# A residual's copy in quarters, and a transfer model in a kernel's own order account

## The chip, the cores and the metric

The kernel runs on one core of a Trainium2 chip. Its time is the device time of one execution in microseconds (us); what counts is the median of several runs. A core has TensorE (PE, matrix products; its weight loads are shown as PEld), VectorE (DVE), ScalarE (ACT), GpSimd (POOL) and SyncE (SP). Each works through its own instructions in order and waits on semaphores. Transfers (DMAs) are issued here by SP, POOL and at the start ACT, and all run on the same 16 DMA engines.

## The reference

Two layers over `x` of 8 images x 256 channels x 32 x 32, in float32. Layer 0 is a convolution and attention hybrid, layer 1 is full attention over the 1024 positions followed by eight experts. Cut to what matters:

```python
# layer 0; the residual is the x on the left
x = x + L0(_gn(x), ...)      # 1x1 products, pooled keys and values (1426 tokens), depthwise 3x3,
                             # layernorm, attention of 8 heads, global-token mix, projection
# layer 1
t = _to_tokens(x)
t = t + L1_attn(_ln_t(t), Wq, bq, Wk, bk, Wv, bv)
t = t + L1_ffn(_ln_t(t), ...)   # 8 experts, three products each, weighted by a softmax gate
x = _from_tokens(t, x)
```

So `t1 = x + L0(...)` is formed for each image, and layer 1 reads it.

## The kernel before

**Stages.** The first stage (to about 1945 us) runs the layer-0 attention of the eight images one after another. Each image `b` has four units, `(c, half)`: four heads `c`, 512 queries `half`. A unit has `NKC` = 12 steps over the keys. In a step PE makes the scores `sc` (four heads, one PSUM tile of four banks), ACT takes the exponential into a tile `pt` (128 x 2048, six buffers), and PE multiplies by the values into `pv`. For each pair of steps `add` (line 1501) has POOL issue a transfer that adds one `pt` to the other in SBUF (`accum_op`); `sums` (line 1508) has DVE add the pairs up, and `normalise` divides. After an image's fourth unit `project` (line 1535) makes the output product and has POOL add it with accumulating stores of 256 KB (`t<-xr`) into `t1[b]` in DRAM.

Everything else of that stage is put between the steps as filler: `prepare(b)` (line 1351) loads the image (`xi`, two halves of 512 KB), normalises, pools and projects it for the next image; `queries` stores `hn<-pool`; `layer1` (line 1599) loads `t1[b]` of a finished image into `t` (1 MB) and makes the second attention's scores and values; `outputs` loads `res`, stores `t2` and `hn`. From about 1970 us the experts run, first with the rest of layer 1 between them, then alone.

**The residual.** `t1[b]` must hold `x[b]` before `project` accumulates into it. For images 0 to 6 `prepare(b)` has SP issue one copy from DRAM to DRAM, 1 MB, right behind the loads of `xi` (lines 1356 and 1357). For the last image `project` loads `x` into SBUF and stores the sum.

**The order account.** The order of each engine's instructions is not written by hand. While the program is built, class `Flow` keeps an account of time: `now` is the time to which each engine is booked, `ready` when each tile is written, `read` when its readers are done. `note` (line 761) books every instruction with a cost from `cost` (line 721; a transfer's issue is 1.0 us on POOL, 0.4 us on SP). Generators (`prepare`, `layer1`, `sums` and so on) say before each piece which engine and tiles they need, and `runnable` (line 837) lets a piece in when the account says that its tiles are there in time: for PE by `at + MARGIN <= until` with `MARGIN` = 1.5, where `until` is about when the PSUM tile of the scores is free. `tile` picks the buffer that is free first. So a booked duration decides where instructions stand in each engine's fixed order; on the chip the engines follow that order and wait on the real semaphores.

For a transfer `note` adds a lag from the end of its issue to its landing, line 799: 2.0 + 0.0045 us for each KB (of 1000 bytes) on SP, 1.5 + 0.0078 on POOL. A transfer's lag doesn't depend on others that are under way.

**The main loop** stands at the end of `attention`: it goes over `steps` (line 1829), calls `scores`, lets filler in with `f.step`, calls `values` for the step before, and `add` after each odd step.

Of the kernel before, what the change touches and what calls it, by code (L numbers as in the profile page):

```python
# [14 lines left out]
DRAM = bass.MemoryType.DRAM  # L15

P = 128
# [7 lines left out]
NKC = 12  # L25
# [26 lines left out]
class Kit:  # L52


    def __init__(self, nc):
        self.nc = nc
        self.n = 0
# [598 lines left out]
class Flow:  # L656
# [27 lines left out]
    def __init__(self, tc, kit):  # L684
        nc = tc.nc
        self.tc, self.kit = tc, kit
        self.now = dict.fromkeys(("PE", "DVE", "ACT", "POOL", "SP"), 0.0)
        self.last = {}
        self.ready, self.read, self.writer, self.reader, self.slots, self.open = {}, {}, {}, {}, {}, set()
        self.pe = self.Engine(self, "PE", nc.tensor)  # L690
        self.ve = self.Engine(self, "DVE", nc.vector)
        self.act = self.Engine(self, "ACT", nc.scalar)
        self.pool = self.Engine(self, "POOL", nc.gpsimd)
        self.sp = self.Engine(self, "SP", nc.sync)
        self.threads = []
        self.cut = {}
        self.also = {}
        self.tiled = None
        self.columns = False
        self.credit, self.port = [0.0, 0.0], 0.0  # L700

    def tile(self, pool, shape, tag, bufs=1):
# [58 lines left out]
    def note(self, engine, op, ins, args, kwargs):  # L761
        aps = [a for a in (*args, *kwargs.values()) if hasattr(a, "tensor") or hasattr(a, "space")]
        out = kwargs.get("out", args[0] if args else aps[0])
        srcs = [a for a in aps if a is not out]
        prev = self.last.get(engine)
        if prev is not None:
            self.tc.add_manual_dep(
                ins.ins,
                prev,
                mybir.DependencyInfo(mybir.DependencyClass.NoSync, mybir.DependencyReason.DATA),  # L770
                reason="program order",
            )
        self.last[engine] = ins.ins.name
        start = self.now[engine]
        names = [n for a in srcs for n in self.keys(a)]
        outs = self.keys(out)
        for n in (*names, *outs):
            if self.writer.get(n) != engine:
                start = max(start, self.ready.get(n, 0.0))
        for o in outs:  # L780
            if self.reader.get(o, engine) != engine:
                start = max(start, self.read.get(o, 0.0))
        cost = self.cost(engine, op, out, srcs)
        if engine == "PE":

            tiling = None if op == "transpose" else self.tiling(srcs)
            if tiling != self.tiled:
                cost += {None: 0.2, "rows": 0.2, "columns": 0.13}[tiling]
                self.tiled = tiling

        wide = [a for a in srcs if a.space != PSUM and a.free_size() > 4]
        if "dma" not in op and engine == "POOL" or engine == "DVE" and wide and (len(wide) > 1 or op in ("tensor_scalar", "tensor_copy")):
            start = max(start, self.port)
            self.port = start + cost
        self.now[engine] = end = start + cost
        lag = 0.15
        if "dma" in op:
            size = 4e-3 * out.shape[0] * out.free_size() if out.space != DRAM else 4e-3 * srcs[0].shape[0] * srcs[0].free_size()
            lag = 2.0 + 0.0045 * size if engine == "SP" else 1.5 + 0.0078 * size
        for n in {*outs, self.key(out)}:  # L800
            self.ready[n] = max(self.ready.get(n, 0.0), end + lag)
            self.writer[n] = "DMA" if "dma" in op else engine
        self.open.difference_update(names)
        for n in {*names, *map(self.key, srcs)}:
            self.read[n] = max(self.read.get(n, 0.0), end + lag)
            self.reader[n] = engine

    @staticmethod
    def key(a):
# [85 lines left out]
def attention(tc, kit, f, outer, ended, nb, consts, x, t1, t2, hn, bounds, vecs, q_t, kv_t, proj_t, gqk_t, wqk, wqkv, vecs1, w1_d, w1c, gate_d, wrc, vecs2, bnvec):  # L895
# [6 lines left out]
    with ExitStack() as ctx:  # L902
        l1, shared = outer
        wp = ctx.enter_context(tc.tile_pool(name="w0", bufs=1))
        work = ctx.enter_context(tc.tile_pool(name="work0", bufs=1))
        psum = ctx.enter_context(tc.tile_pool(name="psum0", bufs=1, space=PSUM))

        def T(pool, shape, tag, bufs=1):
            return f.tile(pool, shape, tag, bufs=bufs)
# [157 lines left out]
        todo, done, read, freed, key_parts, normalised = [], [], [2], [0], [0], [0]  # L1067
# [283 lines left out]
        def prepare(b):  # L1351

            if b:
                yield until(lambda: len(asked) == 4)
            xi = xs.pop(b) if b in xs else load_x(b)
            if b < nb - 1:
                f.sp.dma_start(t1[b], x[b].rearrange("(k p) n -> p k n", p=P))
            st = T(work, [P, 2, 2, 6], "st")
            mv = T(work, [P, 2, 2], "mv")
            for k in range(2):  # L1360
                yield ve(xi[:, k, :])
                for h in range(2):
                    f.ve.bn_stats(st[:, k, h, :], xi[:, k, h * 512 : (h + 1) * 512])
                f.ve.bn_aggr(mv[:, k, :], st[:, k, :, :].rearrange("p h s -> p (h s)"))
            mean, var = mv[:, :, 0], mv[:, :, 1]
            yield pe(mv, tag="sm")
            gm = small()
            f.pe.matmul(gm[:, 0:2], lhsT=grp, rhs=mean, start=True, stop=True)
            yield ve(gm)
            mu = T(work, [P, 2], "mu")  # L1370
            f.ve.tensor_copy(mu, gm[:, 0:2])
            dev = T(work, [P, 2], "dev")
            f.ve.tensor_tensor(dev, mean, mu, ALU.subtract)
            f.ve.tensor_tensor(dev, dev, dev, ALU.mult)
            f.ve.tensor_tensor(dev, dev, var, ALU.add)
            yield pe(dev, tag="sm")
            gv = small()
            f.pe.matmul(gv[:, 0:2], lhsT=grp, rhs=dev, start=True, stop=True)
            yield ve(gv)
            gr = T(work, [P, 2], "gr")  # L1380
            rstd(gr, gv[:, 0:2], 1e-5)
            for k in range(2):
                yield ve(gr)
                f.ve.tensor_scalar(
                    xi[:, k, :], xi[:, k, :], mu[:, k : k + 1], gr[:, k : k + 1], ALU.subtract, ALU.mult
                )
            xl = T(work, [P, 2, NK - HW], "xl")
            if b == 0:
                f.spawn(pool_levels(xi, xl), 2)
            else:  # L1390
                yield from pool_levels(xi, xl)
            xp = xi, xl
            if b == 0:
                todo.extend([None] * 4)
                f.spawn(queries(b, xi), 3)
                yield from first_maps(xp)
            else:
                yield from maps(xp)
            if b:
                yield from queries(b, xi)  # L1400
            made[0] += 1
# [430 lines left out]
        for i in range(len(steps) + 1):  # L1832
            if i < len(steps):
                b, c, half, kc = steps[i]
                sl = slice(half * 512, half * 512 + 512)
                if kc % 4 == 0:
                    f.finish(lambda: key_parts[0] > 3 * b + kc // 4)
                if (half, kc) == (0, 0):
                    f.finish(lambda: (b, c) in qs and (b or (c, 0) in asked))
                    turn[0] = 2 * b + c  # L1840
                    atts[b, c] = T(work, [P, HW], "att", bufs=2)
                if i == 4:
                    f.finish(lambda: {0, 1}.issubset(whole))
                if b == 0 and kc == 0:
                    f.finish(lambda: (c, half) in asked)
                pts[i] = scores(b, c, sl, kc)
                f.step()
            if i:
                b1, c1, half1, kc1 = steps[i - 1]
                if kc1 == 0:  # L1850
                    pv = T(psum, [P, 512], "pv")
                    pairs = []
                    sl1 = slice(half1 * 512, half1 * 512 + 512)
                    f.spawn(unit(b1, c1, sl1, i // NKC, pairs), 0)
                f.finish(lambda: kc1 // 4 in vts[b1])
                values(b1, c1, kc1, pts[i - 1], pv)
                if kc1 % 2:
                    add(kc1, pts.pop(i - 1), pts[i - 2])
                    pairs.append(pts.pop(i - 2))
                if kc1 == NKC - 1:  # L1860
                    f.finish(lambda: projected[0] >= b1)
                    f.act.activation(atts[b1, c1][:, sl1], pv, AF.Copy)
            if i < len(steps):
                f.step((PACE, PACE1))
# [687 lines left out]
```

## Time and profile before

| what | value |
|---|---|
| median of 5 runs | 3311.89 us (3306.25 to 3312.99) |
| the profiled execution | 3312.69 us |
| its span, first to last instruction | 3310.9 us |
| mean granted TensorE clock | 0.978 |
| PE busy | 3103.3 us (94%) |
| DVE busy | 2470.5 us (75%) |
| ACT busy | 1736.0 us (52%) |
| POOL busy | 1220.0 us (37%) |
| transfers issued by POOL, whole span | 179.85 MB, 28.3% of the 16 engines |
| transfers issued by SP, whole span | 181.32 MB, 15.7% of the 16 engines |

The page shows one profiled execution. Its span is the time from the first to the last instruction; the run's own time is 1.8 us longer. Busy slices cut the span in 40 equal parts of 82.8 us and give each engine's busy share in tenths. In views of groups and waits, a line names the engine, the tile it writes, and what ended the idle time before it: `PE sc L669 <- ACT pt L669` means that PE sat idle before writing `sc` until ACT had done with `pt`. L669 is the line of the account's wrapper through which nearly all instructions are issued, so lines say little and tiles say much. A DMA's landing time runs from the start of its issue.

The seven copies of the residual were issued at 1.7, 36.5, 232.6, 409.4, 599.5, 801.4 and 1019.8 us. The four units of image 4, for example, begin at 1052.4, 1127.0, 1177.1 and 1234.3 us.

### The profile page before, as it was taken

The numbers are of one execution on the slowest core, as the hardware profiler recorded it, in microseconds if no ns is written. First come the engines' busy times: TensorE is split into PE (matmuls) and PEld (weight loads), VectorE is DVE, ScalarE is ACT, GpSimd is POOL, SyncE is SP. The second block draws the span as 40 slices with busy tenths as digits, with TensorE's granted clock in tenths as the row PEclk, the third lists the DMA queues.
The fourth block names the chain that finished last, engine by engine and source line by source line (L and its number), as shares of the span: only waits on it lengthen the run. The fifth ranks groups of instructions, "written<-read, shape, count | busy, mean of one in ns | idle before, by whom it ended". The sixth has DMA issues, their size and how long they took to land. (4 is left out here: it accounts for less than half of the span.)

```text
span 3310.9 us, 56919 instructions
## 1 busy us (share of the span) xinstructions
PE 3103.3 (94%) x22906; PEld 1794.4 (54%) x22906; DVE 2470.5 (75%) x4067; ACT 1736.0 (52%) x2329; POOL 1220.0 (37%) x1309
## 2 busy tenths in 40 slices
PE   8788879989999989999989889999999999999998
PEld 4322224334333434334334247777888888888887
DVE  5798989899789869877545545346888887787776
ACT  4466757576766666667565543333333333444443
POOL 2213241420422222211121211006765667777776
PEclk9798989999999999999999999999999999999999
DMA  2265664665655656656666655124444430000000
GB/s 75 70 167 116 137 145 97 136 147 121 131 134 133 121 128 133 135 114 127 145 137 130 135 155 198 58 83 166 140 153 147 143 125 26 20 20 32 20 13 21
DMA packets 111906, 366.89 MB, mean 111 GB/s; under 512 B 13632, under 2 KB 38984, under 8 KB 88400
## 3 DMA queue, kind: packets, MB, share of 16 engines
q0 software_dynamic: 28608, 179.85, 28.3%
q1 hardware_dynamic: 79664, 181.32, 15.7%
q8 instruction: 183, 3.00, 0.4%
q10 hardware_dynamic: 3360, 1.97, 0.2%
q14 instruction: 91, 0.75, 0.1%
HBM read 114.55 MB, written 83.40 MB: 60 GB/s over the span
## 5 line engine op out<-in xcount | busy, mean ns | idle before, releaser
L669 ACT ACTIVATE pt<-sc 128x2048 f32<-128x2048 f32 (+1 forms) x384 | 720.2, 1876 | 302.4 <-PE sc L669 228.4
L669 DVE SCALAR_TENSOR_TENSOR acc<-p,vec,acc 128x961 f32<-128x961 f32 (+3 forms) x960 | 571.4, 604 | 29.5 <-ACT acc L669 3.9
L669 PE MATMUL sc<-q,kn 32*128 32x512 f32 (+1 forms) x3072 | 447.0, 652 | 109.1 <-ACT pt L669 107.8
L669 DVE TENSOR_TENSOR pt<-pt,pt 128x1024 f32<-128x1024 f32 x320 | 387.2, 1254 | 130.9 <-DMA pt<-pt 130.3
L669 POOL DMA_DIRECT2D pt<-pt x192 | 172.9, 900 | 748.9 <-ACT pt L669 633.5
L669 PE MATMUL pv<-pt,vt 128*32 128x512 f32 (+1 forms) x3072 | 420.8, 620 | 1.4 <-ACT att L669 1.4
L669 ACT ACTIVATE p1c<-bank 128x256 f32<-128x256 f32 x229 | 87.5, 382 | 561.0 <-PE bank L669 554.9
L669 ACT ACTIVATE h<-h,bnvec 128x512 f32<-128x512 f32 x458 | 346.5, 805 | 63.0 <-DVE h L669 54.1
L669 POOL TENSOR_TENSOR rstd<-rstd,mhalf 128x4 f32<-128x4 f32 (+2 forms) x88 | 109.6, 1246 | 669.0 <-DVE rstd L669 628.0
L669 DVE TENSOR_TENSOR h<-p1c,bank 128x512 f32<-128x512 f32 x229 | 156.0, 681 | 220.6 <-PE bank L669 209.9
L669 PEld LDWEIGHTS sc<-q,kn 32*128 32x128 f32 (+1 forms) x3072 | 116.2, 178 | 317.2 <-ACT pt L669 206.9
L669 POOL TENSOR_TENSOR tm<-h,tm 128x256 f32<-128x256 f32 x208 | 239.6, 1152 | 16.3
L669 DVE TENSOR_TENSOR h<-u,bank 128x256 f32<-128x256 f32 x458 | 233.2, 550 | 7.9
L669 PEld LDWEIGHTS pv<-pt,vt 128*32 128x32 f32 (+1 forms) x3072 | 60.7, 108 | 304.5 <-issue 287.9
L669 POOL TENSOR_TENSOR tm<-h 128x512 f32<-128x512 f32 x104 | 136.9, 1316 | 195.1 <-ACT h L669 195.1
L669 DVE TENSOR_TENSOR h<-h,gate 128x1024 f32<-128x1024 f32 x128 | 201.6, 1575 | 0.5 <-ACT h L669 0.5
L669 PE MATMUL bank<-h,w2e 128*128 128x256 f32 (+1 forms) x608 | 196.4, 452 | 2.1 <-DVE h L669 1.2
L669 PE MATMUL y<-t,s3e 128*128 128x256 f32 x768 | 187.0, 379 | 4.0 <-POOL t L669 2.1
L669 PE MATMUL bank<-t,s1e 128*128 128x256 f32 x750 | 182.5, 379 | 0.2 <-DVE h L669 0.2
L669 PE MATMUL sm<-y,t 128*32 128x256 f32 (+1 forms) x2144 | 178.7, 382 | 1.4 <-ACT p L669 1.4
L669 PE MATMUL sm<-p,v 128*32 128x256 f32 (+1 forms) x2088 | 177.6, 379 | 0.0
L669 POOL TENSOR_TENSOR t<-h,t 128x256 f32<-128x256 f32 x214 | 170.9, 799 | 16.8
(313 smaller groups left out, 5420.9 us busy)
## 6 DMA issues: line engine op xcount, KB each, us to landing
pt<-pt POOLq DMA_DIRECT2D x160, 1024.0 KB, 7.7
h<-h SPq DMA_DIRECT2D x126, 512.0 KB, 3.3
xi<-in_x_dram SPq DMA_DIRECT2D x16, 512.0 KB, 8.2
t<-t SPq DMA_DIRECT2D x8, 1024.0 KB, 9.3
res<-t SPq DMA_DIRECT2D x32, 256.0 KB, 4.7
t<-res SPq DMA_DIRECT2D x32, 256.0 KB, 4.1
hn<-res SPq DMA_DIRECT2D x32, 256.0 KB, 4.7
hn<-hn SPq DMA_DIRECT2D x16, 512.0 KB, 4.8
```

Of the source, the lines that this page charges most:

```text
L669: ins = fn(*args, **kwargs)
```

## The change

The copy goes out of `prepare`. In the main loop, at step 6 of each unit's 12, SP now issues a quarter: the 128 channels `c` and the 512 positions of that unit, 256 KB, DRAM to DRAM, for images 0 to 6. That makes 28 transfers instead of 7, each of the same image whose unit is running.

In the account the lag of a transfer is no longer fixed. `transfer` keeps two numbers, the work in us that is still left on SP's queue (with the few that ACT issues) and on POOL's. Work is 0.0048 us a KB for POOL's transfers and for those from DRAM to DRAM, 0.0026 for others. Since the last call, `served`, time has gone by: while both queues hold work each is served at half rate, then the one that is left at the full rate. The lag is 1.7, plus what is left on the own queue with the new transfer, plus as much of the other queue's as is served meanwhile; for a transfer that is booked earlier than `served`, the difference is added.

```diff
@@ Flow.__init__
         self.columns = False
+        self.left, self.served = [0.0, 0.0], 0.0
         self.credit, self.port = [0.0, 0.0], 0.0
@@ Flow.note
         lag = 0.15
         if "dma" in op:
+            both = out.space == DRAM and srcs[0].space == DRAM
             size = 4e-3 * out.shape[0] * out.free_size() if out.space != DRAM else 4e-3 * srcs[0].shape[0] * srcs[0].free_size()
-            lag = 2.0 + 0.0045 * size if engine == "SP" else 1.5 + 0.0078 * size
+            lag = self.transfer(engine, end, size * (0.0048 if engine == "POOL" or both else 0.0026))
@@ Flow
+    def transfer(self, queue, at, work):
+
+        span = max(0.0, at - self.served)
+        self.served = max(self.served, at)
+        mine, other = queue == "POOL", queue != "POOL"
+        left = self.left
+        both = 2 * min(left)
+        done = min(span, both) / 2
+        for i in range(2):
+            left[i] = max(0.0, left[i] - done - max(0.0, span - both))
+        left[mine] += work
+        return 1.7 + left[mine] + min(left[mine], left[other]) + self.served - at
@@ prepare(b)
             xi = xs.pop(b) if b in xs else load_x(b)
-            if b < nb - 1:
-                f.sp.dma_start(t1[b], x[b].rearrange("(k p) n -> p k n", p=P))
             st = T(work, [P, 2, 2, 6], "st")
@@ the main loop of attention
                     atts[b, c] = T(work, [P, HW], "att", bufs=2)
+                if kc == NKC // 2 and b < nb - 1:
+                    f.sp.dma_start(t1[b][:, c, sl], x[b, c * P : (c + 1) * P, sl])
                 if i == 4:
```

## The prediction

> **What bounds the kernel now.** I read the page's busy slices first, then the waits of each engine in the attention stage (75 to 1945 us), then stretches of some 30 us where the transfers are thick, then the transfers themselves.
>
> ```profile
> PE   8788879989999989999989889999999999999998
> PEclk9798989999999999999999999999999999999999
> DMA  2265664665655656656666655124444430000000
> ```
>
> PE sets the end: 3103.3 of 3310.9 us are busy, and behind slice 24 (about 2000 us) it hardly idles. The transfers, which are all that this change touches, are thick in slices 2 to 23 only, which is the attention stage. So what can be won or lost is PE's idle time before 2000 us, with the slow clock that follows on it. PE's waits from 75 to 1990 us say what ends that idle time, and the waits of ACT, DVE and POOL (75 to 1945 us) what stands behind:
>
> ```profile
> PE sc L669 <- ACT pt L669: 107.8, 91, 4.4
> ...
> PE sx L669 <- DVE st L669: 8.6, 1, 8.6
> ```
>
> ```profile
> ACT pt L669 <- DMA pt<-pt: 46.9, 15, 5.2
> ...
> DVE pt L669 <- DMA pt<-pt: 127.0, 42, 8.0
> ...
> DVE st L669 <- DMA xi<-in_x_dram: 12.2, 2, 8.1
> ...
> POOL rstd L669 <- DVE rstd L669: 420.2, 72, 15.3
> ```
>
> Columns: total us, times, longest. PE waits for an exponential (`pt`), and the exponential in 15 cases for a `pt` buffer that an accumulating transfer still holds. Where this bites is seen in six stretches (busy us of each engine, then granted clock, share of the DMA engines, GB/s):
>
> ```profile
> core 0: us, PE busy (x) PEld busy (x) DVE busy (x) ACT busy (x) POOL busy (x), PEclk, DMA share, GB/s
> ...
> 409.00:439.00 30.00, 18.48 (x120) 5.97 (x116) 17.48 (x30) 12.36 (x11) 2.59 (x3) 0.83 0.86 224
> 597.00:627.00 30.00, 28.35 (x268) 11.29 (x264) 25.32 (x55) 17.23 (x20) 8.16 (x10) 1.00 0.86 201
> ...
> 1186.00:1216.00 30.00, 22.29 (x158) 7.42 (x154) 17.59 (x42) 20.37 (x23) 8.91 (x11) 0.94 0.78 167
> ...
> 1872.00:1902.00 30.00, 21.05 (x176) 5.34 (x176) 13.37 (x12) 13.98 (x9) 8.29 (x9) 0.83 0.64 128
> ```
>
> 409 and 597 are places of the residual's copy: one loses 11.5 us of PE, the other 1.7 (at 799 and 1018 it is 0 and 0.4). The stretches at 1186 and 1872, and two like them at 1424 (24.46 busy) and 1662 (22.27), hold no copy; together they lose 7.7 + 5.5 + 7.7 + 9.0 = 29.9 us. The stretch from 445 to 480, behind the clash at 409, has PE busy 23.80 of 35: 11.2 lost. POOL shows how the late ones begin:
>
> ```profile
> 1196.79 0.71 POOL L669 TENSOR_TENSOR rstd<-rstd,mhalf 128x2 f32<-128x2 f32 x1 [9.65 <-DVE rstd L669]
> 1197.47 0.88 POOL L669 DMA_DIRECT2D pt<-pt  x1
> ...
> 1198.70 1.19 POOL L669 DMA_DIRECT2D pt<-pt  x1
> ```
>
> POOL stood 9.65 us for a late DVE; two accumulating transfers queued behind it went out 1.2 us apart, the second took 12.4 us, and the exponentials ran out of buffers (4.05 and 3.12 us). It is an error of the written order: the account had DVE earlier than it was.
>
> **The change part by part.** Sizes and landing times in the attention stage:
>
> ```profile
> pt<-pt POOLq DMA_DIRECT2D x160, 1024.0 KB, 7.7
> hn<-pool SPq DMA_DIRECT2D x28, 256.0 KB, 3.5
> ...
> t<-t SPq DMA_DIRECT2D x7, 1024.0 KB, 9.7
> ...
> xi<-in_x_dram SPq DMA_DIRECT2D x12, 512.0 KB, 8.3
> ...
> t<-in_x_dram SPq DMA_DIRECT2D x5, 1024.0 KB, 14.6
> ```
>
> *Issue.* Seven copies become 28 quarters. A copy took 977 ns to issue, a 256 KB store (`t<-res`) 526: 28 x 0.53 - 7 x 0.98 = +8 us on SP, which stood 581 us for `res` alone in this stage. Cost on the path 0; uncovered, 0.5 us of delay for one load a unit. Nothing new waits: the accumulating stores of `project` (first at 362.8 us) need the quarters of their image, the last of which goes out in the middle of its fourth unit (about 313 us for image 0). If that cover went, POOL would stand at line 1557 and the `pt` transfers behind it.
>
> *Copy gone from the head of `prepare`.* At 409 the load of 1 MB `t` (405.0), `hn`, two `xi` and the copy meet three `pt` transfers; the second half of `xi` came 20 us after its issue and DVE, then PE, stood 8.6 us. The copy is queued behind `xi`, so its removal alone need not bring `xi` forward (at 597, with a copy behind, `xi` took 7.5). But the account changes too: it had given each `xi` 2.0 + 0.0045 x 524 = 4.4 us. Now it has 1.7, plus what SP still holds (by then about 4.5: the rest of `t` and `hn`, and 1.36 for each `xi`), plus as much again while POOL holds some (3): some 9 us. PE's matmul then comes 4.6 us later in the order, with other work ahead. Bounds 0 and -11.5; I take -5, nearest to those 4.6. At the start (copies at 1.7 and 36.5 us) PE's first matmul at 8.87 waits for `mv`; I take 0.
>
> *Shorter accumulations in the account.* Before: 1.0 issue + 1.5 + 0.0078 x 1049 = 10.7 us. Now 1.0 + 1.7 + 0.0048 x 1049 = 7.7, more when SP holds work; measured 7.7. The additions in `sums` come some 3 us earlier in DVE's order, and buffers count as free sooner. No row prices an order not yet written; the bounds are the idle time of the stretches that began so, -41.1 (29.9 + 11.2), and the loss in the rival below. The 445 to 480 stretch follows from the clash at 409, so I give back most of it, -8, and of the four others a fifth, -6, since their cause (a late `rstd`) is only indirectly touched.
>
> *Quarters in the middle of units.* Beside a 1 MB copy two `pt` transfers took 9.4 to 12.5 us instead of 7.7, so a copy costs 3.4 to 9.6 us of their lateness, a quarter 0.9 to 2.4. Mostly there is slack; but the stretches at 1186, 1424 and 1662 lie at steps 2 to 10 of a unit, and there the quarter lands: 3 x 0.9 to 2.4 = +2.7 to +7.2. I take +4.
>
> *Loads that now look quicker.* `t` of 1 MB: 7.1 us in the account before, now 0.4 + 1.7 + 2.73 = 4.8, or 7.5 while POOL transfers; measured 9.7, and PE's margin is 1.5. Extra lateness 0 to 2.3 us for 7 loads; with half the time covered by POOL and filler work at hand I take +3 (0 to +16). The weights at 1971 (PE idle 10.1 us there for `w2e`) get 2.8 instead of 3.6: 0, between -3 and +3.
>
> Sum: -5 - 8 - 6 + 4 + 3 = -12. The profiled run has a span of 3310.9 and took 3312.69, 0.8 above the median 3311.89; so 3298.9 us of span, and a median of 3300.
>
> A page against the change: the Trainium skill, "DMA: Bandwidth & Descriptors", section "Bandwidth", says to "Batch DMAs to ≥1 MiB for ≥75% of peak"; its fixed 2.0 us for each DMA ("Anatomy of one DMA") would make four quarters some 6 us dearer than one copy, an estimate, 42 us over the run, all in SP's queue; by it the sum would stay unless those us reach the three tight units. The same fit gives an accumulation 2.0 + 2.4 = 4.4 us, where the row says 7.7; by the page even the new account would be 3 us too slow and the rival below would fall, but the row decides.
>
> **Rivals.** *Slower: the cushion is gone.* The account was 3 us too long for the accumulations, and still DVE waited for them 42 times. At 7.7, the median, half of them come later than written; DVE, in order, stands, the statistics behind it are late, POOL stands at `rstd`, and the next transfers go out in pairs as at 1197. For it: the 420.2 us of `rstd` waits. Against: the account now lengthens an accumulation when SP is busy, which the long ones are. Such a stretch costs 29.9 / 4 = 7.5 us of PE. The other terms being -5 - 8 + 4 + 3 = -6, two more stretches decide (+9). With one more in each of three images that have none: -6 + 22.5 = +16, so 3328.
>
> *No change: transfers were hidden anyway.* Only 46.9 us of ACT's waits are on transfers; filler not done beside them is done after 2000 us at the same price. The clash at 409 is relieved (-5), the quarters cost their lower end (+2.7), the loads nothing: -2.3, so 3310.
>
> *It doesn't do what it says.* SP is in order and stood up to 115.9 us for one store (`hn<-pool`); a quarter behind such a wait is issued with the next burst, as the copy was. Then the quarters cost their upper end, +7.2, beside the -5 of the account: +2, so 3314.
>
> **How the numbers follow.** Forecast (3286 to 3305) 0.47, cushion gone 0.33, hidden 0.14, bunched 0.06. Only about 0.2% (6.6 us) can be told from no change here. Faster 0.48 takes in a little of the hidden case; same 0.19; slower 0.33. The range 3283 to 3332 leaves out the far ends of the first two, about 2 in 10.
>
> **What would show it.** The wait of PE for DVE `st` (8.6) gone and PE busy over 24 in the stretch after the fourth image's `xi` load; the 445 to 480 stretch above 30 of 35. ACT's waits on `pt` transfers under 46.9 if the account helps, over it if the cushion mattered; POOL's pairs of transfers 1.2 us apart fewer or more than the four. DVE's wait on transfers above 200 us would speak for the rival. No SP issue of `t<-in_x_dram` beside `xi`, but 28 spread over the units. I am wrong if PE's idle time before 2000 us grows.

## The result, and the profile after

The changed kernel takes 3316.72 us (median of 30 runs, 3307.32 to 3324.98); beside it the kernel before took 3309.41 us (51 runs). The ratio is 1.0021, with a 95% interval of 1.0015 to 1.0026: 7 us slower, where 12 us faster was forecast. The profiled execution has a span of 3318.7 us, 7.8 above that of before.

The page after, busy slices of PE, the granted clock and the DMA engines:

```profile
PE   8787889999989999989989989999999999999998
...
PEclk9799899999999999999999999999999999999999
DMA  1365655645665565566766746224444440000000
```

PE is as full as before. Its busy time grew by 10.4 us (3103.3 to 3113.7), and its idle time, the sum of the gaps between matmuls, fell from 199.1 to 195.6. What grew can be split at the events that both traces show. The first exponential starts at 83.5 us instead of 81.6 and the last ends at 1954.9 instead of 1943.7: the attention stage is 9.2 us longer. The first expert product comes at 1989.5 instead of 1976.9, and the store of the gate (`gtd`) at 2250.9 instead of 2238.3, both 12.6 late. Of these 12.6 some 5 come back behind the gate, because more expert work was done by then: PE is busy for 1044.9 us from that store to the end, instead of 1049.6.

In the attention stage PE's idle time fell too, 158.2 to 155.0 us, and its busy time grew by 12.5. Part of this is the clock: matmuls that began while half of it was granted take 108.5 us of the stage instead of 89.0 (a `sc` matmul has 0.24 us then, instead of 0.13). At the full clock these 19.5 us more would have taken about half as long, so in this pair of executions some 10 us, an estimate, go with the clock. That the loss as such is the clock isn't shown. Over all executions on record the granted clock has a mean of 0.9783 for the changed kernel (32) and of 0.9789 for the one before (113, beside the experiments), which is some 2 us of a span. In two more draws of the changed kernel (e9 and e10 below) it was 0.0016 and 0.0015 lower than beside them, but with the copy whole (e1 below), which is as slow as the change, 0.0009 higher.

Waits in the attention stage after (75 to 1955 us; total, times, longest):

```profile
PE sc L669 <- ACT pt L669: 118.9, 112, 3.9
```

```profile
ACT pt L669 <- DMA pt<-pt: 35.2, 11, 5.4
```

```profile
DVE pt L669 <- DMA pt<-pt: 177.3, 82, 8.0
```

```profile
POOL rstd L669 <- DVE rstd L669: 442.8, 70, 19.2
```

ACT waits less for a `pt` buffer (46.9 before), DVE much more for an accumulated pair (127.0, 42 times before): the additions stand earlier in DVE's order than their transfers land. The stretches, first after and then before (columns as in the prediction: PE, PEld, DVE, ACT and POOL busy, then granted clock, share of the DMA engines, GB/s):

```profile
405.00:440.00 35.00, 28.24 (x210) 7.97 (x210) 32.03 (x56) 20.32 (x21) 8.63 (x8) 0.95 0.88 209
445.00:480.00 35.00, 33.99 (x322) 12.65 (x318) 28.63 (x33) 19.91 (x20) 22.65 (x26) 0.93 0.50 110
...
930.00:960.00 30.00, 22.96 (x176) 7.49 (x172) 29.23 (x54) 18.60 (x14) 10.54 (x11) 0.97 0.86 185
...
1440.00:1470.00 30.00, 21.92 (x142) 6.49 (x146) 24.49 (x61) 19.19 (x22) 9.65 (x10) 0.89 0.75 158
```

```profile
405.00:440.00 35.00, 21.82 (x148) 7.01 (x148) 22.06 (x45) 15.71 (x12) 2.99 (x4) 0.85 0.86 215
445.00:480.00 35.00, 23.80 (x156) 5.31 (x160) 34.36 (x39) 17.47 (x14) 24.41 (x27) 0.80 0.68 143
```

```profile
930.00:960.00 30.00, 28.34 (x295) 12.37 (x288) 24.19 (x36) 20.17 (x27) 6.33 (x8) 1.00 0.55 138
1440.00:1470.00 30.00, 25.33 (x166) 7.91 (x162) 15.75 (x24) 21.17 (x28) 8.70 (x7) 0.94 0.60 120
```

The clash at the fourth image's load is gone: PE was busy 21.82 of the 35 us from 405 before, now 28.24, and 23.80 of those from 445, now 33.99. New thin stretches came in other places, with a lower clock (930: 5.4 us less PE, 0.97 instead of 1.00). The transfers (KB each, median us to landing):

```profile
pt<-pt POOLq DMA_DIRECT2D x160, 1024.0 KB, 7.7
t<-in_x_dram SPq DMA_DIRECT2D x28, 256.0 KB, 6.5
...
t<-t SPq DMA_DIRECT2D x7, 1024.0 KB, 7.2
...
xi<-in_x_dram SPq DMA_DIRECT2D x12, 512.0 KB, 5.5
```

Loads of `xi` and `t` land sooner (8.3 and 9.7 before), the accumulations as before. SP's queue around the fourth image's load, after and then that load before:

```profile
424.16 0.84 SPq L669 DMA_DIRECT2D xi<-in_x_dram  x2
425.04 0.50 SPq L669 DMA_DIRECT2D t<-in_x_dram  x1
442.90 0.34 SPq L669 DMA_DIRECT2D q<-hn  x1
443.30 1.17 SPq L669 DMA_DIRECT2D t<-in_x_dram  x1
444.52 1.00 SPq L669 DMA_DIRECT2D res<-t  x1
```

```profile
406.78 2.60 SPq L669 DMA_DIRECT2D xi<-in_x_dram  x2
```

Most quarters don't go out in the middle of the units. All 28 follow the SP transfer ahead of them by 0.04 to 0.06 us: a quarter waits for nothing, so SP issues it as soon as the wait ahead of it is over. Beside the exponential of step 6 that is up to 65 us early (243.9 instead of 309.0), and in one case 0.5 late; 11 of the 28 are within 5 us of it.

### The profile page after: what moved, and what is told of

It reads as the page before. It is cut to its first block, busy times and chain, and to the rows that moved or that the text cites. A ratio compares the mean times of both kernels' runs of the same rounds, so it can differ in the third digit from the quotient of the medians.

```text
span 3318.7 us, 56921 instructions
## 1 busy us (share of the span) xinstructions
PE 3113.7 (94%) x22888; PEld 1795.0 (54%) x22888; DVE 2463.4 (74%) x4066; ACT 1735.1 (52%) x2328; POOL 1205.8 (36%) x1303
## 3 DMA queue, kind: packets, MB, share of 16 engines
q1 hardware_dynamic: 82368, 183.42, 16.2%
## 5 line engine op out<-in xcount | busy, mean ns | idle before, releaser
L669 PE MATMUL sm<-p,v 128*32 128x256 f32 (+1 forms) x3048 | 223.0, 381 | 0.2 <-DVE gr L669 0.2
L669 PEld LDWEIGHTS sm<-p,v 128*32 128x32 f32 (+1 forms) x3048 | 141.3, 118 | 92.1 <-issue 32.7
L669 POOL TENSOR_TENSOR t<-h 128x512 f32<-128x512 f32 x106 | 137.0, 1293 | 106.7 <-DVE h L669 83.9
```

The costliest lines, as they stand in the source:

```text
L669: ins = fn(*args, **kwargs)
```

## The experiments

Ratios are to the kernel before, run on the same chip beside them, with 95% intervals. "Booked" is the account's time from the issue of a 1 MB accumulation to its landing: 1.0 for the issue and the lag.

**The two parts alone.** e1 takes `after` and puts the whole copy back behind the `xi` load; e2 takes `before`, with the quarters in the loop:

```diff
 e1: new account, copy whole
+            if b < nb - 1:
+                f.sp.dma_start(t1[b], x[b].rearrange("(k p) n -> p k n", p=P))
-                if kc == NKC // 2 and b < nb - 1:
-                    f.sp.dma_start(t1[b][:, c, sl], x[b, c * P : (c + 1) * P, sl])
 e2: old lags, copy in quarters
-            if b < nb - 1:
-                f.sp.dma_start(t1[b], x[b].rearrange("(k p) n -> p k n", p=P))
+                if kc == NKC // 2 and b < nb - 1:
+                    f.sp.dma_start(t1[b][:, c, sl], x[b, c * P : (c + 1) * P, sl])
```

> The new account with the copy whole, at the head of prepare. Theory A (the account loses: accumulations booked at 7.7 us put DVE's additions too early): about +7 us against the kernel before, ratio 1.002, DVE's wait on pt transfers near 177 us as in the changed kernel. Theory B (the quarters lose, by meeting the accumulating transfers in the middle of units): ratio 1.000 or below, since the xi load is booked better. Theory C (any new order draws anew, whatever the transfers do): anywhere within 0.997 to 1.004, and not the sum of parts.

> The old lags with the copy in quarters at the middle of units. Theory A: ratio 1.000 or below, the clash at the fourth image's load relieved, DVE's wait on pt transfers near 127 us. Theory B: about 1.002, and longer waits of exponentials on pt transfers in the units' second halves. Theory C: anywhere within 0.997 to 1.004.

e1: 3317.28 us, ratio 1.0017 (1.0008 to 1.0026). e2: 3306.69 us, 0.9982 (0.9972 to 0.9992). By this pair the loss goes with the account, and the quarters by themselves do no harm. The clash at the fourth image also belongs to the account: in e1 PE is busy 30.74 of the 35 us from 405, in e2 22.48, as before (21.82). The account brings that gain and loses more elsewhere.

**A cushion for accumulations, and a trifle.** e3 is `after` with POOL's transfers booked 3 us longer; e4 is `before` with SP's fixed lag changed by 0.1 us:

```diff
 e3
-        return 1.7 + left[mine] + min(left[mine], left[other]) + self.served - at
+        return (4.7 if queue == "POOL" else 1.7) + left[mine] + min(left[mine], left[other]) + self.served - at
 e4
-            lag = 2.0 + 0.0045 * size if engine == "SP" else 1.5 + 0.0078 * size
+            lag = 1.9 + 0.0045 * size if engine == "SP" else 1.5 + 0.0078 * size
```

> The changed kernel, but POOL's transfers are booked 3 us longer in the account (4.7 us instead of 1.7 before the work), which gives back the old cushion of 10.7 us. Theory A: the loss goes, ratio to the kernel before 1.000 or below, DVE's wait on pt transfers back to about 127 us. Theory B: 1.002 stays. Theory C: within 0.997 to 1.004 although DVE waits less.

> The kernel before with one trifle: SP's transfers are booked 0.1 us shorter (1.9 for 2.0), the copy as it was. Theories A and B: same time, 0.999 to 1.001, since a tenth of a us is a trifle beside the 3 us of the change. Theory C: moves by as much as the change did, 0.2% or more either way.

e3: 3307.22 us, 0.9983 (0.9974 to 0.9992), and DVE's wait for pairs fell to 75.8 us. e4: 3313.53 us, 1.0002 (0.9993 to 1.0011). Taken by themselves these two speak for the booked length.

**The length alone, in the old account.** e5 books 7.6 us, e6 13.7, with no queues and the copy whole; e7 takes the new account for SP's transfers only; e8 is the trifle the other way:

```diff
-            lag = 2.0 + 0.0045 * size if engine == "SP" else 1.5 + 0.0078 * size
+            lag = 2.0 + 0.0045 * size if engine == "SP" else 1.5 + 0.0049 * size   # e5
+            lag = 2.0 + 0.0045 * size if engine == "SP" else 1.5 + 0.0107 * size   # e6
 e7: e1, and then
+            if engine == "POOL":
+                lag = 1.5 + 0.0078 * size
 e8
+            lag = 2.1 + 0.0045 * size if engine == "SP" else 1.5 + 0.0078 * size
```

> The kernel before with one number of its old account changed: POOL's transfers at 1.5 + 0.0049 us a KB, so that an accumulation of 1 MB is booked at 7.6 us from its issue instead of 10.7; copy whole, no queues. Theory A (the account loses because accumulations are booked too short): ratio about 1.002, DVE's wait on pt transfers 150 us or more. Theory D (the loss is in the queue model itself, its shorter loads of SP or its carry-over between queues, not in POOL's length): 0.999 to 1.001. Theory C (lottery of orders): anything, with no relation to the length.

> The kernel before with POOL's transfers at 1.5 + 0.0107 us a KB: an accumulation is booked at 13.7 us instead of 10.7. Theory A: DVE's wait on pt transfers falls under 127 us; the time stays or falls (0.997 to 1.000) as long as the buffers of pt, which now count as held for longer, do not bind. Theory D: 0.999 to 1.001. Theory C: anything.

> The new account for SP's transfers alone: POOL's lag is the old 1.5 + 0.0078 us a KB again (10.7 us for an accumulation), though its work still counts against SP's queue; the copy whole, as before. Theory A: 1.000 or below. Theory D: 1.002. Theory C: anything.

> The kernel before with SP's transfers booked 0.1 us longer (2.1 for 2.0): a second trifle, to see how far a mere reordering moves the time; the first one moved it by 1.0002. Theories A and D: 0.999 to 1.001. Theory C: 0.2% or more either way.

e5: 3349.53 us, 1.0119 (1.0103 to 1.0134), six times the loss of the change; DVE waits 216.8 us for pairs. e6: 3304.36, 0.9971 (0.9961 to 0.9982), DVE waits 48.4. e7: 3310.48, 0.9996 (0.9987 to 1.0005). By e5 to e7 the account of SP's loads costs nothing, and the loss comes with POOL's length. But e8, a tenth of a us and nothing else, gave 3300.49, 0.9966 (0.9954 to 0.9978): one order's time is a draw, with a scatter of at least 0.3%, and that was against all theories but C. The 1.2% of e5 is clear of such a scatter, the 0.2% between e7 and e1 is not.

**Draws.** To tell a length from a draw, the changed kernel and the cushioned one were drawn twice more, with SP's fixed lag at 1.6 and 1.8:

```diff
-        return 1.7 + left[mine] + min(left[mine], left[other]) + self.served - at
+        return (1.7 if queue == "POOL" else 1.6) + left[mine] + min(left[mine], left[other]) + self.served - at   # e9, e10: 1.8
+        return (4.7 if queue == "POOL" else 1.6) + left[mine] + min(left[mine], left[other]) + self.served - at   # e11, e12: 1.8
```

> The changed kernel with SP's fixed lag 1.6 for 1.7: a trifle, to draw its order anew with accumulations still booked at 7.7 us. Theory A (booked too short): slower than the kernel before, 1.001 or more. Theory C (the +0.2% was one unlucky order): around 0.999 to 1.000 for the mean of the three draws.

> The same with 1.8 for 1.7. Theory A: 1.001 or more. Theory C: the mean of the three draws (the change, this one and the one with 1.6) at 0.999 to 1.000.

> The kernel with the 3 us cushion for accumulations (4.7 for POOL), SP's fixed lag 1.6: its order drawn anew. Theory A: 0.999 or less, and the mean of the three cushioned draws at least 0.002 under that of the three without. Theory C: the two groups overlap.

> The same cushion with SP's fixed lag 1.8. Theory A: 0.999 or less. Theory C: the two groups of three overlap.

e9: 3315.05 us, 1.0010 (0.9999 to 1.0020). e10: 3316.52, 1.0011 (1.0002 to 1.0021). e11: 3298.75, 0.9964 (0.9950 to 0.9977). e12: 3317.24, 1.0022 (1.0013 to 1.0031). The changed kernel's three draws agree (1.0010 to 1.0021); the cushioned ones run from 0.9964 to 1.0022 and overlap them. That the cushion mends the changed kernel isn't shown by these six, and the scatter of a trifle is now 0.6%.

Four more draws: f1 is e5 and f2 is e6 with SP at 1.9, f3 is the quarters with the 13.7 us of e6, f4 the quarters with SP at 2.1 as in e8.

```diff
+            lag = 1.9 + 0.0045 * size if engine == "SP" else 1.5 + 0.0049 * size   # f1
+            lag = 1.9 + 0.0045 * size if engine == "SP" else 1.5 + 0.0107 * size   # f2
+            lag = 2.0 + 0.0045 * size if engine == "SP" else 1.5 + 0.0107 * size   # f3, on e2
+            lag = 2.1 + 0.0045 * size if engine == "SP" else 1.5 + 0.0078 * size   # f4, on e2
```

> Old account, copy whole, accumulations booked at 7.6 us, SP's fixed lag 1.9 for 2.0: the short booking drawn a second time. Theory A: 1.005 or more again. Theory C: anywhere from 0.997 to 1.004, the first 1.0119 having been a stray.

> Old account, copy whole, accumulations booked at 13.7 us, SP's fixed lag 1.9: the long booking drawn a second time. Theory A: 0.999 or less, DVE's wait on pt transfers under 70 us. Theory C: anywhere from 0.997 to 1.004.

> Old account with accumulations at 13.7 us, and the copy in quarters. If both gains are real and add up (0.9982 and 0.9971 alone): about 0.995. Theory C: anywhere from 0.996 to 1.003.

> Old account (10.7 us), the copy in quarters, SP's fixed lag 2.1: the quarters drawn a second time, beside the same nudge with the copy whole, which gave 0.9966. If the quarters help: 0.9966 or less. If their 0.9982 was a draw: anywhere from 0.997 to 1.002.

f1: 3350.28 us, 1.0126 (1.0106 to 1.0145): shortness costs, again. f2: 3309.05, 0.9992 (0.9982 to 1.0003): that length pays beyond 10.7 us isn't shown. f3: 3301.66, 0.9970 (0.9959 to 0.9982), the same as e6 without the quarters. f4: 3293.26, 0.9951 (0.9936 to 0.9966), beside 0.9966 for e8. The quarters gave 0.18%, 0.15% and 0.01% in three pairs; that their sum with the long booking is 0.995 is refuted. None of the three differences is clear of the scatter.

**Which use of the length.** `note` uses a lag twice: `ready` says when the accumulated pair is there (then DVE's addition is let in), `read` when the added `pt` buffer is free again (then an exponential is booked into it). g1 shortens only the first, g2 only the second:

```diff
-        lag = 0.15
+        lag = held = 0.15
 g1
-            lag = 2.0 + 0.0045 * size if engine == "SP" else 1.5 + 0.0078 * size
+            lag = 2.0 + 0.0045 * size if engine == "SP" else 1.5 + 0.0049 * size
+            held = 2.0 + 0.0045 * size if engine == "SP" else 1.5 + 0.0078 * size
 g2
+            held = 2.0 + 0.0045 * size if engine == "SP" else 1.5 + 0.0049 * size
 both
-            self.read[n] = max(self.read.get(n, 0.0), end + lag)
+            self.read[n] = max(self.read.get(n, 0.0), end + held)
```

> The kernel before; only the moment at which an accumulated pair is said to be there is booked short (7.6 us from the issue), the added buffer is held for the old 10.7 us. Theory A1 (DVE's additions come too early in its order): about 1.012, DVE's wait on pt transfers 200 us or more. Theory A2 (buffers count as free too soon, so that the account gives PE less filler between exponentials): 0.998 to 1.002.

> The kernel before; only the added buffer is said to be free early (7.6 us), the accumulated pair is there after the old 10.7 us. Theory A1: 0.998 to 1.002, DVE's wait near 127 us. Theory A2: about 1.012.

g1: 3358.13 us, 1.0150 (1.0134 to 1.0166). g2: 3291.07, 0.9941 (0.9927 to 0.9956), the fastest of all, and lower than either theory had for it. So the loss comes from what is said to be there too early, not from the buffers. g1 shortens that time for all that POOL issues, also for the 28 stores `t<-xr` (by 0.8 us of lag each) and the 32 accumulations of 144 KB (0.4); nearly all of it are the 160 of 1 MB (3.0), but they were not shortened alone. That g2 gains is one draw. DVE's waits in g1 and then g2 (75 to 1945 us):

```profile
DVE pt L669 <- DMA pt<-pt: 241.8, 83, 11.1
```

```profile
DVE pt L669 <- DMA pt<-pt: 100.9, 42, 12.8
```

The timeline of g1 shows how such a wait reaches PE:

```profile
615.00 0.90 POOL L669 DMA_DIRECT2D pt<-pt  x1
...
628.54 2.36 DVE L669 TENSOR_TENSOR pt<-pt,pt 128x1024 f32<-128x1024 f32 x2 [5.34 <-DMA pt<-pt]
...
633.65 0.64 DVE L669 TENSOR_TENSOR res<-res,sm 128x512 f32<-128x512 f32 x1
...
634.34 1.94 PE L669 MATMUL sm<-att,mt 128*32 128x512 f32 x8 [7.23 <-DVE res L669]
```

The accumulations that POOL issued at 615.00 and 622.41 took this long (view of `pt`, 612 to 637 us):

```profile
DMA to landing us min/median/max: 13.4/13.4/13.5
```

DVE stands 5.34 us for the one of 615.00, which landed at 628.41, 13.4 us after its issue, where g1 books 7.6 and the old account 10.7. What stands behind it in DVE's order is late too, among it a reader of a PSUM tile (`res<-res,sm`), and PE stands 7.23 us for that. The `sm` matmuls then run at the half clock (0.50 from 634 to 637 us).

There is another kind. At 1754.23 DVE has done all that stands ahead of its next addition, and POOL issues that pair's transfer only at 1758.24, having waited 9.28 us for an exponential:

```profile
1753.54 0.69 DVE L669 TENSOR_TENSOR att<-att,rec 128x512 f32<-128x512 f32 x1
1765.30 2.36 DVE L669 TENSOR_TENSOR pt<-pt,pt 128x1024 f32<-128x1024 f32 x2 [11.06 <-DMA pt<-pt]
```

```profile
1758.24 0.86 POOL L669 DMA_DIRECT2D pt<-pt  x1 [9.28 <-ACT pt L669]
```

This transfer took 6.9 us: its issue was late for DVE's order, not its landing. Not all of g1's loss goes from DVE to PE at once. PE's idle time in its attention stage is 185.5 us instead of 158.2; what DVE ended grew from 28.0 to 41.6, what ACT ended from 117.9 to 134.2. In e5 and f1 the first fell (22.9 and 25.4) and the second grew alone (141.4 and 139.9). How late additions reach PE by way of ACT isn't shown.

## Why the prediction was wrong, step by step

**The step that failed** is "Shorter accumulations in the account", taken at -8 and -6. It compared the booked 10.7 and 7.7 us with the measured 7.7, called 3 us too long, and counted only what earlier bookings win in stretches that were already seen; what they cost elsewhere stood at nothing in the sum, and only in the rival. A win came: PE is busy 10.2 us more in the 445 to 480 stretch, and 5.2 more in the four others together (at the same times, a rough comparison, since the order has moved). But the short booking by itself gives only 2.1 and 1.8 us in the 445 to 480 stretch (e5 and f1), and the new account without it 3.7 (e7), so it isn't shown that the win is this step's. The cost was what the sum lacked. g1, where additions are let in early and nothing else, shows it with +50 us by its ratio (0.0150 x 3309.91 = 49.6); g2, the other half of the same step, gives 19 back. Both together, the plain short booking, cost 1.2% in both draws.

Two things stood behind the old 3 us. The measured 7.7 is a median: in the changed kernel 79 of the 160 accumulations of 1 MB took longer than 7.75 us, and of DVE's 69 waits for one (157 us, whole run) 41, with 77.5 us, were for these. The other 28, with 80.0 us, were for transfers that landed within 7.75 us: there POOL's issue was late, or DVE early, beside the account's times, which no trace holds. POOL does wait long, 442.8 us for `rstd` alone in the attention stage. In the kernel before it was 11 of 34 waits that were for such quick ones, in g1 30 of 76. So the 3 us covered the spread of the transfers as well as the lateness of their issue.

In the changed kernel most of this loss is not there: its account lengthens an accumulation whenever SP holds work, and it gave 1.0010 to 1.0021 in three draws, and 1.0017 with the copy whole, against 1.0119 and 1.0126 for the plain short booking. That the lengthening is what saves it is likely, but no run takes it out alone.

**The rival "the cushion is gone"** had the cause: at the median, it said, half of the accumulations come later than written, and DVE stands for them. Its way is shown in part only. It sent the loss through POOL (transfers in pairs, buffers short). POOL's wait for `rstd` did grow, 420.2 to 442.8 us and to 496.8 in g1, but transfers less than 2 us apart didn't become more (4 before, 4 after, 5 in g1), and ACT's wait for buffers fell, 46.9 to 35.2 us, and to 27.2 in g1. Part of the loss goes from DVE straight to PE, as in the first timeline above: PE's waits for DVE `res`, `st` and `acc` are 16.5, 10.1 and 8.2 us in g1, against 2.9, 11.1 and 4.1 before. In the changed kernel PE's waits for DVE fell (28.0 to 15.8 us) and those for ACT grew (117.9 to 129.4); the sign that the prediction named for being wrong, more idle time of PE, did not come. Its 3328 was too much.

**The clash at 409** was right: 5 and 8 us were forecast for the two stretches, PE gained 6.4 and 10.2 there. The way is the forecast's in part: DVE's statistics of the image end later than before (433.5 instead of 429.6 us) and PE doesn't stand for them, since other work is ahead. But SP also sends the load 17.4 us later, no longer right behind that of `t`, and its second half lands in 4.7 us instead of 20, which was not foreseen. That the copy's removal alone need not bring it was right too (e2: 22.48 of 35). Another place of the copy, 229 to 259 us, isn't in the prediction's sum; PE lost 8.1 us there before and 8.3 after.

**The quarters** were taken at +4. Alone they brought the ratio down by 0.0015 and 0.0018 in two pairs and 0.0001 in the third, so 0 to -6 us, within the scatter. The rival that they don't do what they say was right about the issue: they leave in SP's bursts, though mostly early, not late. The price it gave to that (+7) was wrong.

**Loads that look quicker** were taken at +3; e7, the new account for SP's transfers alone, is at 0.9996. PE waited 1.7 us for `t` once. The issue cost of 28 quarters, 0, shows nowhere in PE's waits.

The fit of the Trainium skill for a transfer that GpSimd issues ("DMA: Bandwidth & Descriptors", section "Anatomy of one DMA") would have made the rival fall, at 4.4 us for an accumulation, an estimate; measured are 7.7 us, and the rival's cause held. The prediction also put that section's fixed 2.0 us on the quarters, which SP issues; no run here shows a fixed cost of theirs, and the quarters by themselves cost no time.

**What stays open.** The change's 0.2% is smaller than the scatter of a trifle (0.9966 to 1.0002 for 0.1 us either way in the kernel before, 0.9964 to 1.0022 in the cushioned one). That a short booking costs is shown, twice at 1.2% and once at 1.5%. That the +0.2% of this very order is what is left of it, and not a draw, is likely from four draws on one side, and not more than that.

## What to carry to other kernels

In an account from which an order is built, the lag of a transfer has to cover the spread of its length and the lateness of its issue, not only its median; a number fitted to landing times can be right about the transfer and wrong for the order. Additions that came too early on an in-order engine cost more here (1.2 to 1.5%) than those that came too late (0.9971 and 0.9992 with 13.7 us booked), while buffers called free too early cost nothing in one draw: a number for each of the two uses is worth trying. Before a 0.2% difference of such a kernel is explained, draw its order a few times with a trifle changed.

## What was not expected of the hardware

Less idle time didn't mean a better clock. In the changed kernel's profile PE idled 3 us less in the attention stage, yet 19.5 us more of its busy time was on matmuls at the half clock (108.5 against 89.0 us). From 800 to 1000 us its idle time grew from 4.1 to 16.2 us and the granted clock fell from 1.00 to 0.96; but from 600 to 800 us the clock fell from 0.99 to 0.95 while the idle time fell, 15.9 to 13.6. What else decides on the clock isn't shown. And a transfer that waits for nothing is not held until the step that it was written for: all 28 quarters left within 0.06 us of the transfer ahead of them in SP's order, up to 65 us early.
